# Adding a projection in DRAM, holding back query copies and reordering the first image in a list-scheduled attention kernel

## The chip, the cores and the metric

The kernel runs on one core of one Trainium2 chip. The metric is the device time of one execution in microseconds (us), the median of several runs. All profiled executions quoted here are of the fast state. Names: PE is TensorE (PEld its weight loads), DVE is VectorE, ACT is ScalarE, POOL is GpSimd, SP is SyncE, whose queue starts 406 of the 608 transfers that the profile of before lists. An "exp" is the ACT pass that turns one step's attention scores into probabilities.

How the profile's lines are read: L668 or L669 is the helper through which most instructions go, so the tiles tell what an instruction is. `sc` is the tile of the scores, `pt` a tile of probabilities, `sm` and `sx` the PSUM tiles of the background work, `kt` the keys on their way, `xr` the projection's row, `pool` the staging tile of the queries. A line such as `PE sc <- ACT pt: 114.0, 95, 7.1` says that PE, before instructions on `sc`, waited for ACT's on `pt`: us in total, times, longest.

## The reference, cut to what matters

```python
# x: 8 images, 256 channels, 32 x 32
# layer 0: on the group-normalised image
q  = 1x1 conv(x)                              # 8 heads of 32
kv = 1x1 conv(x)
pooled(t): for sides 32, 16, 11, 5: average pool, add depthwise 3x3   # 1426 tokens
k, v = layernorm(pooled(k_map)), layernorm(pooled(v_map))
out  = softmax(q k^T * scale) v               # 1024 queries x 1426 keys per head
out  = proj(mix(out)) + proj_b                # mix: a small 32 x 32 attention per head
x = x + out
# layer 1: attention over each image's 1024 tokens, then 8 experts of three products each
```

Layer 0 makes 384 steps of attention: 8 images, 2 groups of 4 heads, 2 halves of the queries, 12 chunks of keys.

## The kernel before: the parts that matter

The program orders its own instructions. While it is built, a small model of the engines (`Flow`) keeps the expected time of each engine and of each tile. The attention steps are the fixed backbone; convolutions, projections and layer 1 are background threads. A thread hands over what it needs next (`yield pe(tile, tag="sm")`: PE, these tiles ready, a PSUM tile free), and the model decides between which two attention steps the group goes. What it decides, the order of each engine's list, is fixed at build time.

```python
FILLER, PACE, PACE1, CAP, MARGIN, LANDING = 5, 4.0, 2.0, (1.5, 1.5), 1.5, 9.5

def note(...):                     # after every instruction: when will its output be there?
    lag = 0.15
    if "dma" in op:
        lag = 3.0 if engine == "SP" else LANDING
    ...

def runnable(self, need, rank=0):  # may this thread's next group go in here?
    ...
    return (not self.closed
            and (self.credit[rank >= FILLER] > 0 or pe < until - 0.5)
            and at + MARGIN <= until and slot <= until)

def scores(b, c, sl, kc):          # one attention step; ONE PSUM tile "sc", 6 tiles "pt"
    t = T(psum, [P, 4, 512], "sc")
    ... 4 matmuls ...
    pt = T(work, [P, 4, 512], "pt", bufs=6)
    f.act.activation(pt[:w], t[:w], AF.Exp, scale=SCALE0)

def project(b):
    for m in range(2):
        for half in range(2):
            xt = T(work, [P, 512], "xr")                          # one tile
            f.sp.dma_start(xt, x[b, m * P : (m + 1) * P, sl])     # image row in
            yield pe(atts[b, 0], atts[b, 1], tag="sm")
            ... 2 matmuls into ps ...
            yield ve(ps, xt)
            f.ve.scalar_tensor_tensor(xt, ps, bias[:, m:m+1], xt, ALU.add, ALU.add)
            f.sp.dma_start(t1[b][:, m, sl], xt)

# queries of images 2 to 8: product, copy by ACT into the one "pool" tile, store to DRAM
yield pe(xi, tag="sm")
ps = small()
... 2 matmuls ...
q = T(work, [P, 512], "pool")                                     # taken after the matmul
f.act.activation(q, ps, AF.Copy, scale=...)
f.sp.dma_start(hn[b][:, c, sl], q)
```

Every second step's probability tile is added to the one before it by an accumulating transfer of POOL (`pt<-pt`, 1024 KB, landing 7.3 us after its issue in before, median), and is free for a new exp only when that has landed: ACT stood 45.6 us in 15 places of before for it.

## Time and profile before

| | before |
|---|---|
| time, median of 4 runs | 3413.79 us (3412.46 to 3414.23) |
| PE idle, 0 to 160 us | 160 − 102.03 = 58.0 us |
| PE idle, 160 to 2052 us (rest of attention) | 1892 − 1761.12 = 130.9 us |
| first, ninth exp | 105.99, 162.72 us |

The stretches of the second and third row come from a table of stretches of the kernel before. The columns are the stretch, its length, busy us (with the number of instructions) of PE, PEld, DVE, ACT and POOL, the granted TensorE clock, DMA share and GB/s:

```profile
0.00:160.00 160.00, 102.03 (x366) 48.38 (x367) 98.75 (x253) 64.43 (x110) 42.16 (x64) 0.83 0.22 57
160.00:2052.00 1892.00, 1761.12 (x9918) 793.52 (x9917) 1424.95 (x2459) 1163.51 (x1385) 405.99 (x473) 0.97 0.59 133
```

PE is at work 93% of the second stretch, so there is no large hole to close: what can be gained lies in a start that is a third idle and in many small waits.

### The profile page before, as it was taken

What the parts mean: (1) busy time and instruction counts of PE and PEld (TensorE: products, weight loads), DVE (VectorE), ACT (ScalarE), POOL (GpSimd) and SP (SyncE); (2) the same over time, 40 slices, a digit from 0 to 9 for tenths busy, and PEclk for the clock granted to TensorE, in tenths of its full rate; (3) what the DMA queues carried; (4) which work ended last, traced back from release to release, by engine and by line L of the source; (5) the groups of instructions that cost most, each with busy time, mean ns of one, the idle gap of its engine ahead of it and who ended that gap; (6) DMA issues with size and microseconds to landing.
All of it is one profiled execution on the core that took longest, in us unless ns stands there. A gap on an engine that the chain in (4) does not pass through costs nothing.

```text
span 3418.4 us, 39922 instructions
## 1 busy us (share of the span) xinstructions
PE 3204.7 (94%) x15264; PEld 1781.8 (52%) x15264; DVE 2285.8 (67%) x3914; ACT 1675.6 (49%) x2193; POOL 499.0 (15%) x616
## 2 busy tenths in 40 slices
PE   7588899999999899999999989998999999999998
PEld 3232244444444334434434356646777777777776
DVE  6587798888888878888644543216776666666665
ACT  3466667566676576566664523342223333333332
POOL 3122213122141221321211200004000000000000
PEclk9699999999999999999999999999999999999999
DMA  1257565555555655555665663123440000000000
GB/s 48 63 114 165 135 135 115 125 126 123 138 116 122 161 108 128 127 122 129 148 134 132 141 191 124 56 77 132 140 160 31 19 29 27 19 19 19 19 13 20
DMA packets 105032, 337.47 MB, mean 99 GB/s; under 512 B 12976, under 2 KB 38328, under 8 KB 81600
## 3 DMA queue, kind: packets, MB, share of 16 engines
q0 software_dynamic: 24576, 172.51, 25.8%
q1 hardware_dynamic: 76896, 160.35, 13.6%
q8 instruction: 122, 2.00, 0.2%
q10 hardware_dynamic: 3360, 1.97, 0.2%
q14 instruction: 78, 0.64, 0.1%
HBM read 98.33 MB, written 63.97 MB: 47 GB/s over the span
## 4 chain that ended last, share of the span: by engine, by line
PE 74%; DMA 5%; ACT 4%; DVE 2%; issue 2%; POOL 1%; SPq 0%; ACTq 0%; DVEq 0%; POOLq 0%
PE bank L669 25%; PE sm L669 18%; PE y L669 11%; PE sc L669 8%; PE sx L669 6%; PE pv L669 6%; ACT pt L669 3%; DMA pt<-pt 2%; DMA t<-xr 1%; DMA xr<-in_x_dram 1%; DVE acc L669 0%; DMA hn<-hn 0%; DVE pt L669 0%; DVE rec L669 0%; DVE xr L669 0%
## 5 line engine op out<-in xcount | busy, mean ns | idle before, releaser
L669 ACT ACTIVATE pt<-sc 128x2048 f32<-128x2048 f32 (+1 forms) x384 | 720.7, 1877 | 317.1 <-PE sc L669 244.7
L669 PE MATMUL sc<-q,kn 32*128 32x512 f32 (+1 forms) x3072 | 452.4, 659 | 115.5 <-ACT pt L669 114.0
L669 DVE SCALAR_TENSOR_TENSOR acc<-p,vec,acc 128x225 f32<-128x225 f32 (+7 forms) x928 | 528.5, 576 | 35.7 <-ACT acc L669 11.2
L669 PE MATMUL bank<-h,w2e 128*128 128x512 f32 x1024 | 480.5, 595 | 0.0
L669 ACT ACTIVATE h<-bank,bnvec 128x512 f32<-128x512 f32 x302 | 233.1, 772 | 484.5 <-PE bank L669 464.4
L669 DVE TENSOR_TENSOR pt<-pt,pt 128x1024 f32<-128x1024 f32 x320 | 390.0, 1261 | 84.8 <-DMA pt<-pt 82.6
L669 PE MATMUL pv<-pt,vt 128*32 128x512 f32 (+1 forms) x3072 | 422.6, 623 | 0.0
L669 ACT ACTIVATE h<-c,bnvec 128x512 f32<-128x512 f32 x210 | 159.6, 807 | 318.6 <-DVE c L669 318.6
L669 POOL DMA_DIRECT2D pt<-pt x192 | 169.8, 884 | 923.2 <-ACT pt L669 788.8
L669 DVE TENSOR_TENSOR c<-p1c,bank 128x512 f32<-128x512 f32 x105 | 72.2, 688 | 314.9 <-PE bank L669 314.9
L669 PEld LDWEIGHTS sc<-q,kn 32*128 32x128 f32 (+1 forms) x3072 | 117.8, 181 | 311.5 <-ACT pt L669 209.4
L669 PEld LDWEIGHTS bank<-h,w2e 128*128 128x128 f32 x1024 | 194.8, 191 | 153.0 <-issue 141.4
L669 PEld LDWEIGHTS pv<-pt,vt 128*32 128x32 f32 (+1 forms) x3072 | 61.0, 109 | 306.6 <-issue 291.4
L669 POOL TENSOR_TENSOR rstd<-rstd,mhalf 128x4 f32<-128x4 f32 (+2 forms) x88 | 107.0, 1216 | 733.8 <-DVE rstd L669 593.7
L669 DVE TENSOR_TENSOR h<-h,gates 128x1024 f32<-128x1024 f32 x128 | 156.9, 1226 | 71.3 <-DMA h<-h 64.2
L669 PE MATMUL bank<-hn,w1e 128*128 128x256 f32 (+1 forms) x604 | 192.7, 448 | 10.1 <-DMA hn<-hn 10.1
L669 PE MATMUL y<-t,s3e 128*128 128x256 f32 x768 | 187.1, 380 | 0.0
L669 PE MATMUL sm<-p,v 128*128 128x256 f32 x736 | 173.8, 388 | 6.1 <-DVE xr L669 6.1
L669 ACT ACTIVATE p<-sm 128x512 f32<-128x512 f32 (+1 forms) x154 | 89.9, 584 | 173.7 <-PE sm L669 134.2
L669 PE MATMUL sm<-y,t 128*128 128x256 f32 x712 | 169.4, 385 | 2.1 <-ACT p L669 2.1
L669 PEld LDWEIGHTS bank<-hn,w1e 128*128 128x128 f32 x604 | 114.7, 191 | 99.9 <-issue 92.4
L669 PEld LDWEIGHTS sm<-p,v 128*128 128x128 f32 x736 | 139.3, 193 | 49.7 <-issue 24.4
(294 smaller groups left out, 4624.9 us busy)
## 6 DMA issues: line engine op xcount, KB each, us to landing
pt<-pt POOLq DMA_DIRECT2D x160, 1024.0 KB, 7.3
h<-h SPq DMA_DIRECT2D x80, 512.0 KB, 3.4
xi<-in_x_dram SPq DMA_DIRECT2D x16, 512.0 KB, 5.0
t<-t SPq DMA_DIRECT2D x8, 1024.0 KB, 6.9
res<-t SPq DMA_DIRECT2D x32, 256.0 KB, 4.4
t<-res SPq DMA_DIRECT2D x32, 256.0 KB, 2.6
hn<-res SPq DMA_DIRECT2D x32, 256.0 KB, 3.4
hn<-hn SPq DMA_DIRECT2D x16, 512.0 KB, 5.8
```

What stands on the lines that cost most here:

```text
L669: ins = fn(*args, **kwargs)
```

## The change

Its intent: (1) no engine waits for an image row to land, because the image is copied to its place in DRAM ahead of time and the projection is added to it there by a transfer; (2) a query product isn't started before its staging tile is free, so ACT doesn't stand behind a transfer; (3) the first scores come earlier: keys' maps first, their tiles taken from layer 1's space so that the probability tiles stay free; and the model's landing times are made to grow with the size of the transfer.

```diff
-LANDING = 9.5
 ...
-            lag = 3.0 if engine == "SP" else LANDING
+            size = 4e-3 * out.shape[0] * out.free_size() ...      # KB
+            lag = 2.0 + 0.0045 * size if engine == "SP" else 1.5 + 0.0078 * size
 ...
 def first_maps(xp):
-    for m in (2, 3, 0, 1):         # values first; maps 0 and 1 and a sum in "pt" tiles
+    for m in range(4):             # keys first; two "pt" tiles, sums in "kn" and layer 1's "v"
 ...
-    f.spawn(first_keys(), 5)       # all four key convolutions as one thread
+    f.spawn(first_keys(0), 1)
+    f.spawn(first_keys(1), 5)
 ...
 def prepare(b):
+    if b:
+        yield until(lambda: len(asked) == 4)
     xi = xs.pop(b) if b in xs else load_x(b)
+    if b < nb - 1:
+        f.sp.dma_start(t1[b], x[b].rearrange("(k p) n -> p k n", p=P))
 ...
 def queries(b, xi):
-    yield pe(xi, tag="sm")
+    q = T(work, [P, 512], "pool") if b else qs[b, c][:, sl]
+    yield pe(xi, q, tag="sm")
 ...
 def project(b):
-    f.sp.dma_start(xt, x[b, m * P : (m + 1) * P, sl])
-    yield pe(atts[b, 0], atts[b, 1], tag="sm")
+    yield pe(atts[b, 0], atts[b, 1], xt, tag="sm")
     ...
-    yield ve(ps, xt)
-    f.ve.scalar_tensor_tensor(xt, ps, bias[:, m : m + 1], xt, ALU.add, ALU.add)
-    f.sp.dma_start(t1[b][:, m, sl], xt)
+    yield act(ps)
+    f.act.activation(xt, ps, AF.Identity, bias=bias[:, m : m + 1])
+    yield pool(xt)
+    f.pool.dma_start(out=t1[b][:, m, sl], in_=xt, accum_op=ALU.add)
 ...
-f.finish(lambda: key_parts[0] > 1)                  # first score after two groups of keys
+f.finish(lambda: key_parts[0] > 0)                  # after one
 ...
+    if i == 4:                                      # fifth score: key maps' small taps must be placed
+        f.finish(lambda: {0, 1}.issubset(whole))
```

(Cut: the last image keeps the old projection; the queries of the first image are a thread of their own, and so are its groups of value tokens; the diagonals of the first convolutions and the projection weights move to other tiles of layer 1.)

More of the change, by code (lines that the diff above doesn't have):

```diff
@@ L783, in note @@
         if "dma" in op:
-            lag = 3.0 if engine == "SP" else LANDING
+            size = 4e-3 * out.shape[0] * out.free_size() if out.space != DRAM else 4e-3 * srcs[0].shape[0] * srcs[0].free_size()
+            lag = 2.0 + 0.0045 * size if engine == "SP" else 1.5 + 0.0078 * size
         for n in {*outs, self.key(out)}:
@@ L925, in attention @@
         gqkw = weight(gqk_t, "y", 512, l1)
-        pjw = weight(proj_t, "v", 256, l1)
+        pjw = T(l1, [P, 2, C], "p1", bufs=6)
+        nc.scalar.dma_start(pjw, proj_t.rearrange("(k p) f -> p k f", p=P))
         con = kit.con
@@ L1113, in attention @@
         f.split(pmap, 512, HW)
-        first, large, whole, pooled = {}, [], [], []
+        first, large, whole, pooled, asked = {}, [], [], [], []
         def first_diagonals():
             middle = T(l1, [P, 2, P], "rec1")
-            rest = T(work, [P, 4, 512], "pt", bufs=6).rearrange("p a (b q) -> p (a b) q", q=P)
+            rest = T(l1, [P, 16, P], "t")
             first["diag"] = middle, rest
@@ L1128, in first_maps @@
         def first_maps(xp):
-            for m in (2, 3, 0, 1):
-                c = m % 2
-                if m == 2:
-                    p, acc = pmap, T(work, [P, NK], "acc", bufs=3)
-                elif m == 3:
+            for m in range(4):
+                if m < 2:
                     p = T(work, [P, 4, 512], "pt", bufs=6).rearrange("p j q -> p (j q)")
+                    acc = T(l1, [P, NK], "v") if m else T(work, [P, NK], "kn", bufs=3)
+                else:
+                    p = T(work, [P, NK], "acc", bufs=3) if m == 3 else pmap
                     acc = T(work, [P, NK], "acc", bufs=3)
-                else:
-                    both = T(work, [P, 4, 512], "pt", bufs=6).rearrange("p j q -> p (j q)")
-                    p = both
-                    acc = T(work, [P, 4, 512], "pt", bufs=6).rearrange("p j q -> p (j q)")
                 for t in (p, acc):
@@ L1145, in first_maps @@
                 first[m] = p, acc
-            for s0, w in KEY_SLICES:
-                if s0 >= HW:
+            for m, s0 in [(m, s0) for g in (0, 2) for s0 in (0, 512) for m in (g, g + 1)] + [(m, HW) for m in range(4)]:
+                if s0 == HW:
                     yield until(lambda: pooled)
-                for m in (2, 3, 0, 1):
-                    c = m % 2
-                    p, acc = first[m]
-                    src = source(xp, s0, w)
-                    yield pe(src, tag="sm")
-                    ps = small()
-                    for k in range(2):
-                        f.pe.matmul(
-                            ps[:, :w],
-                            lhsT=kvw[:, k, m * P : (m + 1) * P],
-                            rhs=src[:, k, :],
-                            start=k == 0,
-                            stop=k == 1,
-                        )
-                    f.act.activation(p[:, s0 : s0 + w], ps[:, :w], AF.Copy)
-                    for s, n in enumerate(SIDES):
-                        a, z = max(OFFS[s], s0), min(OFFS[s] + n * n, s0 + w)
-                        if a < z and (m >= 2 or s):
-                            f.act.activation(
-                                acc[:, a:z],
-                                ps[:, a - s0 : z - s0],
-                                AF.Identity,
-                                bias=db(c, s),
-                                scale=mid[:, c * 4 + s : c * 4 + s + 1],
-                            )
-                if s0 == 512:
@@ new lines, in first_maps @@
+                w = min(512, NK - s0)
+                c = m % 2
+                p, acc = first[m]
+                src = source(xp, s0, w)
+                yield pe(src, tag="sm")
+                ps = small()
+                for k in range(2):
+                    f.pe.matmul(
+                        ps[:, :w],
+                        lhsT=kvw[:, k, m * P : (m + 1) * P],
+                        rhs=src[:, k, :],
+                        start=k == 0,
+                        stop=k == 1,
+                    )
@@ new lines, in first_maps @@
+                f.act.activation(p[:, s0 : s0 + w], ps[:, :w], AF.Copy)
+                for s, n in enumerate(SIDES):
+                    a, z = max(OFFS[s], s0), min(OFFS[s] + n * n, s0 + w)
+                    if a < z and (m >= 2 or s):
+                        f.act.activation(
+                            acc[:, a:z],
+                            ps[:, a - s0 : z - s0],
+                            AF.Identity,
+                            bias=db(c, s),
+                            scale=mid[:, c * 4 + s : c * 4 + s + 1],
+                        )
@@ L1175, in first_maps, with first_keys @@
+                if (m, s0) == (3, 512):
                     large.append("maps")
-                    f.spawn(first_keys(), 5)
+                    f.spawn(first_keys(0), 1)
+                    f.spawn(first_keys(1), 5)
             whole.append("maps")
-        def first_keys():
+        def first_keys(half):
             n = SIDES[0]
             middle, rest = first["diag"]
-            for half in range(2):
-                for m in range(2):
-                    p, acc = first[m]
-                    pin = p[:, : n * n].rearrange("p (h w) -> p h w", h=n)
-                    yield pe(p[:, : n * n], middle, rest, tag="sm")
-                    ps = small()
-                    pout = ps.rearrange("p (h w) -> p h w", w=n)
-                    for i, tap in enumerate((4, 0, 1, 2, 3, 5, 6, 7, 8)):
-                        dy, dx, y0, y1, x0, x1 = windows(tap, n)
-                        y0, y1 = max(y0, 16 * half), min(y1, 16 * half + 16)
-                        f.pe.matmul(
-                            pout[:, y0 - 16 * half : y1 - 16 * half, x0:x1],
-                            lhsT=rest[:, 8 * m + i - 1, :] if i else middle[:, m, :],
-                            rhs=pin[:, y0 + dy : y1 + dy, x0 + dx : x1 + dx],
-                            start=i == 0,
-                            stop=i == 8,
-                        )
-                    f.act.activation(acc[:, half * 512 : half * 512 + 512], ps, AF.Identity, bias=db(m, 0))
-                large.append(("keys", half))
@@ new lines, in first_keys @@
+            for m in range(2):
+                p, acc = first[m]
+                pin = p[:, : n * n].rearrange("p (h w) -> p h w", h=n)
+                yield pe(p[:, : n * n], middle, rest, tag="sm")
+                ps = small()
+                pout = ps.rearrange("p (h w) -> p h w", w=n)
+                for i, tap in enumerate((4, 0, 1, 2, 3, 5, 6, 7, 8)):
+                    dy, dx, y0, y1, x0, x1 = windows(tap, n)
+                    y0, y1 = max(y0, 16 * half), min(y1, 16 * half + 16)
+                    f.pe.matmul(
+                        pout[:, y0 - 16 * half : y1 - 16 * half, x0:x1],
+                        lhsT=rest[:, 8 * m + i - 1, :] if i else middle[:, m, :],
+                        rhs=pin[:, y0 + dy : y1 + dy, x0 + dx : x1 + dx],
+                        start=i == 0,
+                        stop=i == 8,
+                    )
+                f.act.activation(acc[:, half * 512 : half * 512 + 512], ps, AF.Identity, bias=db(m, 0))
@@ L1203, in taps @@
+            large.append(("keys", half))
         def taps(c, s, p, acc):
@@ L1376, in prepare @@
                 todo.extend([None] * 4)
+                f.spawn(queries(b, xi), 3)
                 yield from first_maps(xp)
@@ L1379, in prepare, with queries @@
                 yield from maps(xp)
+            if b:
+                yield from queries(b, xi)
+            made[0] += 1
+        def queries(b, xi):
             for c in range(2):
@@ L1395, in prepare @@
                         )
-                    q = T(work, [P, 512], "pool") if b else qs[b, c][:, sl]
                     f.act.activation(q, ps, AF.Copy, scale=vec[:, V_NW + c : V_NW + c + 1])
@@ L1399, in prepare @@
                         f.sp.dma_start(hn[b][:, c, sl], q)
-            made[0] += 1
+                    else:
+                        asked.append((c, half))
         def fetch_queries():
@@ L1440, in keys_and_values @@
             vts[b] = {}
-            if b == 0:
-                for g in range(2):
-                    yield from value_tokens(b, g)
-            else:
-                for g in range(3):
-                    f.spawn(value_tokens(b, g), 2)
+            for g in range(3):
+                f.spawn(value_tokens(b, g), 2)
+            if b:
                 yield until(lambda: len(vts[b]) == 3)
@@ L1449, in keys_and_values @@
                 yield until(lambda: len(done) >= 4 * b + 4)
-            for g in range(2 if b == 0 else 3):
+            for g in range(3):
                 yield from key_tokens(b, g)
             if b == 0:
-                yield from value_tokens(b, 2)
-                yield from key_tokens(b, 2)
+                yield until(lambda: len(vts[b]) == 3)
                 freed[0] += 1
@@ L1520, in project @@
                     sl = slice(half * 512, half * 512 + 512)
-                    if b == nb - 1:
-                        xt = last[:, m, sl]
-                    else:
-                        xt = T(work, [P, 512], "xr")
-                        f.sp.dma_start(xt, x[b, m * P : (m + 1) * P, sl])
-                    yield pe(atts[b, 0], atts[b, 1], tag="sm")
+                    xt = last[:, m, sl] if b == nb - 1 else T(work, [P, 512], "xr")
+                    yield pe(atts[b, 0], atts[b, 1], xt, tag="sm")
                     ps = small()
@@ L1531, in project @@
                         )
-                    yield ve(ps, xt)
-                    f.ve.scalar_tensor_tensor(xt, ps, bias[:, m : m + 1], xt, ALU.add, ALU.add)
-                    if b < nb - 1:
-                        f.sp.dma_start(t1[b][:, m, sl], xt)
+                    if b == nb - 1:
+                        yield ve(ps, xt)
+                        f.ve.scalar_tensor_tensor(xt, ps, bias[:, m : m + 1], xt, ALU.add, ALU.add)
+                    else:
+                        yield act(ps)
+                        f.act.activation(xt, ps, AF.Identity, bias=bias[:, m : m + 1])
+                        yield pool(xt)
+                        f.pool.dma_start(out=t1[b][:, m, sl], in_=xt, accum_op=ALU.add)
             if b == nb - 1:
@@ L1815, in attention @@
                 if (half, kc) == (0, 0):
-                    f.finish(lambda: (b, c) in qs)
+                    f.finish(lambda: (b, c) in qs and (b or (c, 0) in asked))
                     turn[0] = 2 * b + c
                     atts[b, c] = T(work, [P, HW], "att", bufs=2)
+                if i == 4:
+                    f.finish(lambda: {0, 1}.issubset(whole))
+                if b == 0 and kc == 0:
+                    f.finish(lambda: (c, half) in asked)
                 pts[i] = scores(b, c, sl, kc)
```

## The prediction

> **What bounds the kernel now.** I read the page first: TensorE (PE) is busy 3204.7 of 3418.4 us (94%), VectorE (DVE) 67%, ScalarE (ACT) 49%, and the chain that ended last is PE for 74% of the span. So the time is PE work plus PE idle, and the question is where PE's 214 us of idle lie. The second view is the table of stretches; columns are the stretch, its length, busy us of PE, PEld, DVE, ACT, POOL, then granted clock, DMA share and GB/s.
>
> ```profile
> 0.00:85.00 85.00, 62.20 (x168) 30.49 (x168) 55.71 (x118) 32.38 (x69) 26.95 (x44) 0.97 0.15 48
> 85.00:171.00 86.00, 50.83 (x236) 22.58 (x236) 45.40 (x139) 38.63 (x51) 15.21 (x21) 0.70 0.29 63
> ...
> 1026.00:1368.00 342.00, 323.17 (x1797) 147.89 (x1795) 282.40 (x519) 216.64 (x273) 75.17 (x87) 0.99 0.58 130
> ...
> 2394.00:3418.00 1024.00, 1010.39 (x3876) 735.85 (x3874) 642.88 (x1002) 334.08 (x521) 0.00 (x0) 0.99 0.12 43
> ```
>
> The first 171 us hold 58 us of PE idle, at a clock of 0.70 in the second half. From about 340 us PE is 92 to 96% busy, and the experts after 2394 us, which the change doesn't touch, leave 14 us. The third view is who PE waited for:
>
> ```profile
> PE sc L669 <- ACT pt L669: 114.0, 95, 7.1
> PE sx L669 <- ACT kt L669: 12.5, 1, 12.5
> PE sm L669 <- DVE xr L669: 12.3, 3, 6.1
> PE sm L669 <- ACT kt L669: 11.3, 3, 6.4
> ...
> PE sm L669 <- ACT pool L669: 2.3, 1, 2.3
> ```
>
> The first row is mostly not a fault to be mended here: the scores have one PSUM tile, so a step of attention takes score 1.1 us plus exp 1.88 us plus handover, 3.15 us, and where nothing is put between, PE idles 1.0 us. I counted such bare steps in the order of PE's instructions: 64 of 384 before, 65 after. That part stays.
>
> How the start looks, in order of time:
>
> ```profile
> 105.99 1.88 ACT L669 ACTIVATE pt<-sc 128x2048 f32<-128x2048 f32 x1
> 128.35 1.88 ACT L669 ACTIVATE pt<-sc 128x2048 f32<-128x2048 f32 x1 [6.43 <-DMA pt<-pt]
> 134.01 1.88 ACT L669 ACTIVATE pt<-sc 128x2048 f32<-128x2048 f32 x1 [3.64 <-DVE pt L669]
> 143.87 1.88 ACT L669 ACTIVATE pt<-sc 128x2048 f32<-128x2048 f32 x1 [7.98 <-DMA pt<-pt]
> 162.72 1.88 ACT L669 ACTIVATE pt<-sc 128x2048 f32<-128x2048 f32 x1 [1.43 <-PE sc L669]
> ```
>
> These are the first, fifth, sixth, seventh and ninth exp. The first image's maps fill the six probability tiles, so exps wait for tiles. The ninth needs the third group of keys, which needs all small convolution taps on DVE. And the two waits that the change names, a projection and a query copy:
>
> ```profile
> 1367.91 0.75 DVE L669 SCALAR_TENSOR_TENSOR xr<-sm,mtb,xr 128x512 f32<-128x512 f32 x1 [2.94 <-DMA xr<-in_x_dram]
> 1368.72 3.78 PE L669 MATMUL sm<-xi,qw 128*128 128x512 f32 x4 [6.00 <-DVE xr L669]
> ...
> 287.05 0.69 ACT L669 ACTIVATE pool<-sm,vec 128x512 f32<-128x512 f32 x1 [2.67 <-DMA hn<-pool]
> 287.64 1.87 ACT L669 ACTIVATE pt<-sc 128x2048 f32<-128x2048 f32 x1
> 289.56 1.14 PE L669 MATMUL sc<-q,kn 32*128 32x512 f32 x8 [2.05 <-ACT pt L669]
> ```
>
> In the first, DVE stands at the head of its queue until the image row has landed, the PSUM tile stays taken, PE stands 6.00 us. In the second, ACT stands until the one staging tile has left, the exp behind it is late, PE stands 2.05 us.
>
> [...] This trace has only accumulates in SBUF (the probability tiles: 1024 KB, 7.3 us to landing); none into DRAM, so that cost is my estimate. [...] here the DMA share is 0.56 to 0.62 in most of attention, so there is room. [...] granted clock 0.70 in the stretch with idle gaps of 12.5, 7.1, 6.4 and 6.4 us. [...]
>
> **The change, part 1: projection in DRAM.** It removes 28 additions on DVE (0.745 us each, 20.9 us), 28 loads of 256 KB and 28 stores, and adds 28 ACT copies with bias (an ACT pass over 128x512 with scale takes 0.69 us: 19.3 us), 28 GpSimd issues (0.86 us each as for the probability tiles: 24 us on an engine busy 15%) and 7 copies of 1 MB from DRAM to DRAM. The copies are issued one image ahead, on the sync queue. Bytes stay the same: the copy replaces the load, the accumulate the store. An accumulated byte takes more engine time: 25.8% of the span for 172.51 MB against 13.6% for 160.35 MB, 1.8 times as much per byte; 7.3 MB of it is about 1% of the span, off the path. On PE's path lies only the wait: 12.3 us (6.1 + 6.0 + 0.2). DVE's 20.9 us is beside PE and frees little; ACT's 19.3 us lands on an engine busy 63% there and can delay an exp by 0.7 us now and then, of 28 perhaps a third on the path, 5 us. Net −12.3 + 5 = about −7, −12 at best.
>
> **Part 2, queries held back.** ACT waited 38.1 us in 16 places for the staging tile. I laid these beside PE's gaps of over 0.3 us: PE stood in four places, 2.05, 0.42, 2.33 and 0.68 us, 5.5 us. All of it should go, since the matmul is now not issued before the tile is expected free: −5.
>
> **Part 3, the start.** By the order of instructions. PE now does four query and eight map groups first: 12 × 1.72 us (four matmuls at 0.43) from 14.35, to 35. Then two convolutions of 7.4 us, to 50. DVE starts its 16 large taps (1.27 us) at 35 instead of 26, has 15 done at 54, then the first keys' statistics, the second image's statistics, and the 16th tap at about 63.5. The value transposes wait for that, then the last key convolution (7.4 us) ends at 73, ACT normalises the keys behind it, transposes, first score at about 78, first exp after two table loads (2.6 us) at about 81 instead of 106.
>
> But that is not the gain. Four exps then go without waiting for a tile; the sixth and seventh take the tiles of the key maps and wait for DVE's taps, as the waits in the built program confirm. DVE's small taps took from 52.25 to 133.9 before, 81.7 us. After, that stretch loses a statistics chain (3.6 us) and about 6 us of waits, and takes in layer 1's weight preparation (4.5 us of copies and scalings, 8.0 us for the batch norm vectors with their GpSimd waits): 84.6 us, from 63.5 to 148. Behind it come the third keys' transposes, one sum of 2.35 us, statistics, normalisation, transposes, some 13 us: the ninth exp at about 161 to 163, against 162.72. What is gained is what PE did by then: eight groups of layer-1 weight products (1.9, 2.0, 0.95, 0.95, 2.0 and three of 1.9 us, 13.4 us) stand before the ninth score now, and stood behind it, in a stretch where PE was full (9.0 and 10 of 10 us from 170 to 190). DVE gets a similar lead. So −14, and the first score 25 us earlier mostly buys idle time.
>
> **Sum.** −7 −5 −14 = −26; better landing estimates (2.7 instead of 9.5 us for the 18-row adds, 6.7 instead of 3.0 for large loads) should take a few of the 16 us in which PE stood because an exp waited for a tile's DMA (2.8 to 3.9 us each): −3. 3413.5 − 29 = 3384.
>
> **Rivals.** (a) The first score's 25 us arrive whole at the end: for it, PE idles 58 us there and the clock is low; against it, the tap count on DVE is the same and DVE must finish before the ninth exp. It would give about 3360. (b) The waits on xr only change place: layer 1's load of t1 must wait for the last accumulate, GpSimd's queue holds the probability adds behind an accumulate that waits for ACT, and the one xr tile now serialises four chunks. For it, one tile and a queue in order; against it, chunks are spread and layer 1 is filler. It would leave part 1 at zero or +8: 3392 to 3400. (c) The 1 MB copy, issued right behind the first image, slows the first weights: landing near 9.4 us, needed at 14.35; a miss costs 1 to 4 us. (d) The reordering of some 1,500 us of background work is luck of ±8 us either way.
>
> **Range and chances.** Good: −24 −12 −6 −10 = 3362. Bad: −3 −6 −2 = 3402. 2% is 68 us, 39% of the 175 us of idle before 2052 us that isn't the first load; I give that 4%. Slower by 2% has no mechanism: 1%.
>
> **What would show it.** First exp near 81, sixth and seventh waiting for DVE, ninth near 162; layer-1 weight products before 160 us; no PE wait on DVE xr, and under 3 us on its successor; ACT's wait for the staging tile under 8 us; PE idle from 400 to 2000 us down by 10 to 20 us; total PE busy unchanged within 20 us. I am wrong if the ninth exp comes 15 us earlier (rival a), if exps wait longer for tiles because accumulates crowd the adds, or if PE waits at the load of t1.

## The result, and the profile after

| | before | after |
|---|---|---|
| time, median of 4 runs each | 3413.79 us | 3382.82 us (3382.07 to 3386.29) |
| ratio | | 0.9912 (0.9895 to 0.9929) |
| PE idle, 0 to 160 us | 58.0 us | 43.6 us |
| PE idle, 160 to 2052 us | 130.9 us | 113.9 us |

A ratio is the mean time of one kernel's fast runs over the mean of the other's in the same rounds, so it is not quite the ratio of the medians.

The result is 31.0 us faster, 0.9%, well clear of the noise; predicted were 29. (It is less than 2%, which the record's class calls "same"; the prediction gave this 95%.) The idle of PE before 2052 us fell by 14.4 + 17.0 = 31.4 us. That this is so near to 31.0 is chance: the two profiled executions differ by 38.5 us (spans of 3418.4 and 3379.9 us; that of before took 3420.16 us, 6 us above its median), of which PE's idle in the whole span is 28.8 us and its busy time 9.7 us. The table of stretches of the changed kernel, columns as before:

```profile
0.00:160.00 160.00, 116.40 (x436) 60.65 (x440) 100.52 (x268) 67.42 (x117) 45.12 (x66) 0.86 0.28 76
160.00:2052.00 1892.00, 1778.15 (x10005) 806.47 (x9998) 1420.32 (x2458) 1191.58 (x1427) 428.76 (x505) 0.98 0.61 133
```

PE does 14.4 us more before 160 us. ACT has 28 us more in the second stretch, mostly its 28 copies of the projection; POOL has 23 us more, the issues of the new adds.

The exps of the start, in order of time (start, duration, engine, operation, tiles, and in brackets how long ACT stood idle before and for what): first, fifth, sixth, seventh, ninth.

```profile
82.01 1.88 ACT L668 ACTIVATE pt<-sc 128x2048 f32<-128x2048 f32 x1
...
143.83 1.88 ACT L668 ACTIVATE pt<-sc 128x2048 f32<-128x2048 f32 x1 [0.67 <-PE sc L668]
146.97 1.88 ACT L668 ACTIVATE pt<-sc 128x2048 f32<-128x2048 f32 x1 [1.26 <-PE sc L668]
...
151.79 1.88 ACT L668 ACTIVATE pt<-sc 128x2048 f32<-128x2048 f32 x1 [0.46 <-PE sc L668]
...
161.53 1.88 ACT L668 ACTIVATE pt<-sc 128x2048 f32<-128x2048 f32 x1 [1.30 <-PE sc L668]
```

The first exp comes 24 us earlier and the ninth 1.2 us earlier. Between the fourth (93.44 us) and the fifth lie 50 us. The sixth and seventh don't wait for DVE here; they wait for their own scores.

Who PE waited for, in us in total, times, and the longest:

```profile
PE sc L668 <- ACT pt L668: 92.9, 96, 3.2
...
PE sx L668 <- DVE rec L668: 8.0, 1, 8.0
...
PE sm L668 <- DVE p L668: 6.7, 2, 6.0
PE sx L668 <- DMA res<-in_w_dram: 4.7, 1, 4.7
PE sm L668 <- ACT kt L668: 4.3, 9, 1.5
PE sx L668 <- ACT kt L668: 3.6, 5, 2.9
```

The waits on the projection's row (`DVE xr`, 12.3 us) are gone, and so is the one on the query copy (`ACT pool`, 2.3 us). PE's waits for ACT's work on the keys (`ACT kt`), the largest of the old start, fell from 12.5 + 11.3 to 3.6 + 4.3 us. Three new ones are in the start: PE stands at groups of the mixing matrix (`rec`, `p`) and of layer 1's weights (`res`) that its order puts ahead of the fifth score. And what touched the projection's tile:

```profile
L668 POOL DMA_DIRECT2D t<-xr x28: 863/882/931, 346.5 to 1810.8; - x28
...
  POOL t L668: 113.7, 23
  PEld sc L668: 0.2, 1
...
DMA to landing us min/median/max: 4.3/4.7/5.8
```

The first row is POOL's issues (ns, minimum, median, maximum; first and last start). The next two are who waited for an instruction on this tile: POOL stood 113.7 us for ACT's copies, but none of these issues is in the chain of work that ended last, and PE's weight loads lost 0.2 us. The add of 256 KB into DRAM lands after 4.7 us.

Of the signs that I named, two are missing: the sixth and seventh exp, and the idle of PE from 400 to 2000 us, which fell by 7.4 us (82.0 to 74.6) and not by 10 to 20. The second is partly a matter of the window: in after it takes in PE's wait before the experts' first products (10.98 us, ending at 1997.70 us), which in before ends at 2014.84 us. The other signs are there. It remains to be seen whether each part of the change gives what I put down for it.

### The profile page after: what moved, and what is told of

Read it like the earlier page. It is cut to its first block, busy times and chain, and to the rows that moved or that the text cites. A ratio compares the mean times of both kernels' runs of the same rounds, so it can differ in the third digit from the quotient of the medians.

```text
span 3379.9 us, 39921 instructions
## 1 busy us (share of the span) xinstructions
PE 3195.0 (95%) x15270; PEld 1780.3 (53%) x15270; DVE 2267.8 (67%) x3890; ACT 1695.4 (50%) x2222; POOL 520.7 (15%) x644
## 3 DMA queue, kind: packets, MB, share of 16 engines
q10 hardware_dynamic: 3360, 1.97, 0.2%
## 4 chain that ended last, share of the span: by engine, by line
PE 66%; ACT 2%; issue 2%; DMA 1%; DVE 1%; POOL 1%; SPq 0%; POOLq 0%; ACTq 0%; DVEq 0%
PE bank L668 25%; PE sm L668 14%; PE y L668 11%; PE sc L668 6%; PE sx L668 6%; PE pv L668 5%; ACT pt L668 2%; DMA pt<-pt 1%; POOL rstd L668 0%; DVE t L668 0%; DMA h<-h 0%; DMA hn<-hn 0%; POOL pt L668 0%; DVE rec L668 0%; DMA t<-pt 0%
## 5 line engine op out<-in xcount | busy, mean ns | idle before, releaser
L668 PE MATMUL sc<-q,kn 32*128 32x512 f32 (+1 forms) x3072 | 444.8, 649 | 94.2 <-ACT pt L668 92.9
L668 PE MATMUL sm<-y,t 128*128 128x256 f32 x752 | 180.4, 385 | 0.0
L668 PEld LDWEIGHTS sm<-y,t 128*128 128x128 f32 x752 | 137.9, 190 | 56.1 <-issue 34.4
L668 PE MATMUL bank<-t,s1e 128*128 128x256 f32 x636 | 154.7, 379 | 2.8 <-DVE t L668 2.8
```

Source lines behind the costliest of these rows:

```text
L668: ins = fn(*args, **kwargs)
```

## The experiments

Twelve kernels were run, in three groups; each group ran on one chip beside the kernel before, whose medians were 3414.8, 3413.4 and 3413.6 us. Theory A is the prediction: each part has its own gain and the gains add up (−7, −5, −14, −3). Theory B is my rival (d), made larger: where the background groups fall is luck, and worth more than the parts. Theory C is that the parts move waits to other places.

### One part alone

`e1_dram_only`: the kernel before with the changed `project` and the copy in `prepare`, and

```diff
-            lag = 3.0 if engine == "SP" else LANDING
+            lag = 3.0 if engine == "SP" else 3.5 if out.space == DRAM else LANDING
```

This second line was needed. With 9.5 us put down for the new adds, too, the model placed the projection so late that a check of the built program found the attention tile read after a later image's had replaced it. The landing estimates are thus no separate nicety: part 1, as it is written here, can't be built safely on the old one.

> The kernel before with part 1 alone (projection copied by ACT, added to the image in DRAM; the old landing estimates stay, except 3.5 us for the new adds into DRAM). My prediction gives -7 us, so about 3406.5 us, with PE's 12.3 us of waits on the image row gone and first exp unchanged near 106 us. Rival (b), the wait only changes place: 3413 to 3421 us. Rival (d), reordering is luck: anything within 8 us of 3413.5, and PE's idle moves in stretches where no projection stands.

Measured: 3414.02 us against 3414.8, ratio 0.9998 (0.999 to 1.0006). PE's waits on the image row are gone, and nothing is gained. In the profile PE idles 126.6 us from 160 to 2052 us (before: 130.9).

`e2_held_only`: the kernel before with

```diff
-                    yield pe(xi, tag="sm")
+                    q = T(work, [P, 512], "pool") if b else qs[b, c][:, sl]
+                    yield pe(xi, q, tag="sm")
                     ...
-                    q = T(work, [P, 512], "pool") if b else qs[b, c][:, sl]
```

> The kernel before with part 2 alone (query copies of images 2 to 8 issued when the staging tile is free). Prediction: ACT's 38.1 us of waits for the staging tile fall under 8 us, PE gains 5 us: about 3408.5 us. Rival: the waits were off the path, 3412 to 3415 us with ACT's wait still gone. Rival (d), luck: up to 8 us either way.

Measured: 3456.30 us, ratio 1.0124: 42 us slower. ACT's wait for the staging tile is 0, as expected, so the part does what it is meant to do. What it costs is not at that tile: PE idles 150.8 us from 160 to 2052 us, 20 us more than before, at waits in many places (image rows 19.0 us instead of 12.3, layer 1's load of the image 11.4 instead of 2.1). (The window leaves out this kernel's wait before the experts' first products, 6.1 us, and holds that of before, 10.1 us; without these two it is 30 us more.)

`e3_start_only`: the changed kernel with the old `project`, `queries` and landing estimates, so the kernel before with part 3 alone.

> The kernel before with part 3 alone (keys first, other tiles for the first image's maps, split first keys; old landing estimates, old projection, queries not held). Prediction: first exp near 82 us, ninth near 162 us, -14 us in all: about 3399.5 us, with PE idle before 160 us down by 14 us. Rival (a), the first exp's 24 us arrive whole: about 3388 us. Rival: the products of layer 1 moved ahead were free before as well, then 3410 to 3414 us.

Measured: 3418.28 us, ratio 1.001 (1.0003 to 1.0017). Its table of stretches:

```profile
0.00:160.00 160.00, 118.13 (x444) 60.89 (x448) 101.06 (x269) 67.85 (x118) 45.05 (x66) 0.86 0.25 65
160.00:2052.00 1892.00, 1753.21 (x9880) 786.50 (x9873) 1436.46 (x2450) 1159.30 (x1380) 401.57 (x471) 0.98 0.58 130
```

First exp 81.3 us, ninth 159.9. In its own stretch the part gives 16.1 us of PE idle (58.0 − 41.9), as predicted. In the rest PE idles 138.8 us, 7.9 more than before, and no gain is left at the end.

`e4_landing_only`: the kernel before with the two new `lag` lines alone.

> The kernel before with the new landing estimates alone. Prediction: -3 us, about 3410.5 us, and ACT waits less for probability tiles whose add has not landed (45.6 us in 15 places before). Rival: this is the larger part of what came from 400 to 2000 us, -10 us or more, 3403 us or less. Rival (d), luck: within 8 us either way, with that wait unchanged.

Measured: 3430.17 us, ratio 1.0045 (1.0033 to 1.0058), 15 us slower. The exps' waits for a tile whose add had not landed did fall, from 29.4 to 24.2 us from 160 to 2052 us. PE's idle in that stretch rose to 148.4 us.

Four parts that are each 0 to 42 us slower by themselves, and 31 us faster together: theory A doesn't hold in its simple form. Either the parts need each other, or something else decides between kernels of this kind.

### Nothing of the change: neighbours

To see what placing alone does, I changed a number that is no property of the chip: `MARGIN`, by which an operand must be expected ready before its group is put between two scores. The order of PE's instructions in the built program is then the same for a stretch at its beginning and another from there on.

```diff
-MARGIN = 1.5
+MARGIN = 1.4        # n_before_14, n_after_14;  1.6 in n_before_16, n_after_16
```

> The kernel before with nothing of the change; the margin by which an operand must be ready before a group is put between two scores goes from 1.5 to 1.4 us, which means nothing for the hardware but puts most of the background work in other places. Theory 'the placing is luck and before stood on a lucky one': 10 to 40 us slower, 3424 to 3455 us, as e2 (+42) and e4 (+15) were. Rival 'each part of the change has its own cost, placing is worth under 8 us': 3406 to 3421 us.

> The same with 1.6 us. Luck theory: 3424 to 3455 us. Rival: 3406 to 3421 us. If one neighbour is faster than before by more than 5 us, before was not a lucky placing.

> The changed kernel with the same margin 1.4 us. If the change has a gain of its own and before and after are equally tuned, this neighbour is as far above 3382.8 us as before's neighbours are above 3413.5 us (gap of the means of neighbours 20 to 35 us). If after is only a lucky placing, it falls among before's neighbours, at 3415 us or more. If placing is worth little, 3375 to 3391 us.

> The changed kernel with 1.6 us. The same three outcomes: a gap to before's neighbours of 20 to 35 us (own gain), none (luck), or 3375 to 3391 us (placing worth little).

Measured:

| kernel | time, us | PE idle 0 to 160 | PE idle 160 to 2052 | span profiled | PE busy in it |
|---|---|---|---|---|---|
| before | 3413.4 | 58.0 | 130.9 | 3418.4 | 3204.7 |
| n_before_14 | 3427.9 | 57.8 | 126.4 | 3431.6 | 3220.7 |
| n_before_16 | 3453.8 | 57.9 | 165.3 | 3455.7 | 3210.8 |
| after | 3382.8 | 43.6 | 113.9 | 3379.9 | 3195.0 |
| n_after_14 | 3404.3 | 43.3 | 128.0 | 3400.6 | 3202.9 |
| n_after_16 | 3385.3 | 42.9 | 106.8 | 3380.4 | 3206.1 |

The time is a median; the other columns are of one profiled execution. After itself wasn't run again in this group.

The tenth of a microsecond that means nothing costs 14.5 and 40.4 us beside before, and 21.5 and 2.5 us beside after. Each of the two kernels is the fastest of its three. The table of stretches of the slowest, n_before_16, and then who its PE waited for:

```profile
0.00:160.00 160.00, 102.09 (x367) 48.26 (x367) 98.69 (x253) 64.62 (x110) 41.93 (x64) 0.83 0.23 57
160.00:2052.00 1892.00, 1726.68 (x9762) 763.51 (x9761) 1418.69 (x2425) 1153.56 (x1365) 406.36 (x469) 0.97 0.57 128
```

```profile
PE sc L669 <- ACT pt L669: 134.0, 111, 7.1
...
PE sx L669 <- DMA t<-t: 10.9, 3, 4.9
...
PE sx L669 <- POOL tst L669: 6.1, 1, 6.1
```

The start is the same to 0.1 us. Behind it PE does 34 us less in the same time. It waits at more scores for the exp before (111 times against 95, 20 us more). Attention steps with no background group between them explain little of that: in the built programs there are 67 against 64. A few groups stand at a worse place: PE waits 10.9 us in three places of one PSUM tile for layer 1's image load (and 4.2 us in one of the other), and 6.1 us for POOL's `tst`. Behind the start no one of these waits is longer than 6.1 us; it is their sum that is large.

Idle is not all. n_before_14 has 2.8 us less PE idle in its whole span than before and is still 13.2 us longer in the profile: PE is busy 16.0 us more, with practically the same products to do. In the six kernels this busy time differs by up to 26 us. The granted clock is 0.972 to 0.974 in the profiles of before's three and 0.977 to 0.980 in those of after's, and the profiles of before and after hold 15264 and 15270 matmuls; what makes the difference has not been followed.

The families don't overlap: the three placings of before have the mean 3431.7 us, those of after 3390.8. The gap is 40.9 us. Between the profiled executions it is 48.3 us, of which the start's stretch holds 14.6 (mean idle 57.9 against 43.3), the rest of attention 24.6 (140.9 against 116.2) and PE's busy time 10.7. The standard deviations are 20.5 and 11.8 us, so three against three gives the gap with a standard error of about 14 us (the root of a third of the sum of their squares), and a 95% interval would reach down to about zero. Theory B in its strong form, the change is only a lucky placing, is unlikely by this; the kernels of the next group make it weaker still. But of the single comparisons of one kernel with another, those above included, none under some 20 us says much.

### All but one part

`e5_no_dram` (the changed kernel with the old `project`, without the copy), `e7_no_held` (the tile `q` taken after the matmul again), `e8_no_start` (the kernel before with parts 1, 2 and the estimates).

```diff
 # e5: as the change's diff of project and prepare, reversed
 # e7
-                    q = T(work, [P, 512], "pool") if b else qs[b, c][:, sl]
-                    yield pe(xi, q, tag="sm")
+                    yield pe(xi, tag="sm")
                     ...
+                    q = T(work, [P, 512], "pool") if b else qs[b, c][:, sl]
 # e8: first_maps, first_keys, keys_and_values, the tiles and the finish conditions as before
```

> The changed kernel without part 1 (projection added by DVE, image rows loaded, no copy of 1 MB). If part 1 has a gain of its own of 7 us or more, this stands above the mean of after and its two neighbours (3382.8, 3404.3, 3385.3; mean 3391): 3398 us or more, with PE waits of 5 to 13 us on the image row back, which the three kernels without part 1 have (12.3, 4.8, 7.0 us) and the three with it have not. If part 1 gives nothing, it lies between 3380 and 3405 us like those three.

Measured: 3395.34 us, 4.5 above the mean of the after family. PE waits on the image row are back, 1.6 + 2.7 = 4.3 us. By what was put down beforehand that is the outcome for no gain (3380 to 3405 us); but a gain of that size would fit the spread as well.

> The changed kernel without part 2 (query copies issued before the staging tile is free). ACT's waits for that tile come back, 38 to 54 us as in all kernels without it. If they cost what I predicted, PE stands 2 to 5 us for them and the time is 5 us above the mean of 3391 us; if the many late exps behind them cost more, 15 us or more above, 3406 us or later; if nothing, 3380 to 3405 us.

Measured: 3403.74 us, 12.9 above the family's mean and within its range. ACT's waits (engine, tile, releaser, us, times, longest) are back:

```profile
ACT pool L668 <- DMA hn<-pool: 43.5, 17, 6.5
```

PE itself stood 2.8 + 0.2 us for that tile. The 5 us of the prediction and the 13 of the time can't be told apart at this spread.

> The changed kernel without part 3 (parts 1 and 2 and the new landing estimates on the kernel before). First exp near 106 us and PE idle before 160 us near 57 us, as in all kernels with the old start (54 to 58), against 43 in all with the new. Time 14 us above the mean of 3391 us, 3405 us, give or take the placing (20 us); idle from 400 to 1800 us as in the three changed ones (52 to 64 us) if the rest of the gain comes from parts 1 and 2 and the estimates, 66 us or more (as in the kernels of before, 66 to 107) if it comes with the start.

Measured: 3388.30 us, 2.5 *below* the family's mean. This was my largest miss in the expectations. The first exp is at 107.16 us, as in all with the old start, but the stretch reads otherwise:

```profile
0.00:160.00 160.00, 115.74 (x442) 54.98 (x443) 107.56 (x261) 75.05 (x122) 43.52 (x65) 0.88 0.28 75
160.00:2052.00 1892.00, 1767.08 (x9969) 807.15 (x9968) 1418.68 (x2448) 1185.14 (x1421) 434.14 (x502) 0.98 0.61 134
```

PE idles 44.3 us before 160 us, as little as with the new start. The ninth exp is what moved:

```profile
139.11 1.88 ACT L668 ACTIVATE pt<-sc 128x2048 f32<-128x2048 f32 x1 [2.16 <-PE sc L668]
...
145.03 1.88 ACT L668 ACTIVATE pt<-sc 128x2048 f32<-128x2048 f32 x1 [0.62 <-PE sc L668]
```

It comes at 145.03 instead of 162.72 us. In the kernel before, the fifth and seventh exp stood 6.43 and 7.98 us for a tile's add to land, and DVE's last small tap ended at 133.9 us; here the waits of the fifth to eighth are at most 2.16 us (the fourth waits 5.67 us for DVE), the taps end at 122.6 us, and DVE stands less (busy 107.6 us before 160 us, against 98.8). Which moved group began it I have not followed. The estimates alone don't do it (e4: ninth exp at 163.7 us, idle 55.2 us). So the start's 14 us can be had in two ways, by more work before a ninth exp at 162 us (part 3) or by an earlier ninth exp with the old start. With parts 1, 2 and the estimates there, part 3 gives nothing that these runs show; but this is one placing, so only to some 20 us. The idle from 400 to 1800 us, the other thing that was put down, is 62.0 us, inside the 52 to 64 of the three changed kernels (before: 69.0); e5 and e7 have 65.9 and 66.8, so it does not tell the parts apart.

### What the start's gain is made of

`e12_weights_late`: the changed kernel with the mixing matrix and layer 1's weights begun after the third group of keys.

```diff
-f.spawn(chain(mix(), weights1(), outputs()), 5)
-f.spawn(layer1(), 6)
     ...
+                if i == 8:
+                    f.spawn(chain(mix(), weights1(), outputs()), 5)
+                    f.spawn(layer1(), 6)
```

> The changed kernel with the mixing matrix and layer 1's weight products begun only after the third keys are there. DVE then has none of their work and waits between 88 and 137 us (about 10 us of work, 13 us of waits), so the ninth exp should come near 138 us instead of 161.5. My prediction says that the start's gain is the PE work done before the ninth score: then this is a wash, the 20 us of PE work move behind it, PE idle before the ninth score stays 40 to 44 us, and the time is that of after give or take the placing (3375 to 3410 us). Rival (a), an earlier ninth exp is worth its whole time: 3360 to 3365 us, and this is the faster kernel. Rival: the ninth exp stays near 160 us because something else holds it, then 3400 us or more.

Measured: 3400.31 us. The ninth exp:

```profile
143.52 1.88 ACT L668 ACTIVATE pt<-sc 128x2048 f32<-128x2048 f32 x1
```

Its PE up to the end of the ninth score (columns as in the tables of stretches):

```profile
0.00:142.00 142.00, 94.42 (x348) 41.78 (x350) 96.01 (x233) 62.90 (x108) 39.49 (x64) 0.88 0.27 73
```

The exp is 18.0 us earlier than after's (I had expected 23), and the time is 9.5 us above the family's mean, within its range. PE idles 47.6 us up to the ninth score, where 40 to 44 were expected (after: 43.6 in 160 us), and 49.2 us before 160 us. An earlier ninth exp is not worth its own length: rival (a) asked for 3360 to 3365 us. The time to the ninth exp shrinks by what DVE no longer does, and PE has as much less done by then: 94.4 us of work in 142 us, where after's PE has done 116.4 us in 160. This is about the wash that the prediction's view of the start implies. It is also the one candidate for a faster kernel that these readings suggested, and it isn't faster. The fastest kernels measured are the changed one and its neighbour n_after_16.

### What was not run

What this paragraph says of builds is the author's account; the record holds no run of them. The direct rival to part 1, the old addition with the matmul held until the image row has landed, didn't pass the check of races with one row tile, and the build had no room for two; a mended form passed but was not among the twelve. The changed kernel with the old landing estimates (and 3.5 us for the new adds) was built and not run either. Nor were kernels with two of the four parts, or neighbours of those with one.

## Why the prediction was right, point by point

**The total.** 3384 us predicted, 3382.8 measured. The 14 us of the start are seen where they were predicted. The other 15 are not shown part by part, and that the sum came within 1.2 us is partly luck: against the families' means the gap is 41 ± 14 us, with which the predicted 29 agree. Had the change been made with the neighbour's 1.4 us, its 3404.3 us would have been 20 us from my number and outside my range.

**What bounds the kernel.** Held. PE's waits for the exp at scores from 160 to 2052 us were 94.2 us in 89 places and are 89.3 in 91. Bare steps stayed, as counted.

**Part 1, −7.** The wait is gone in all kernels with it (0 us), and is 2.4 to 19 us in those without, on the sum of both PSUM tiles, by placing. It only partly changed place: POOL stands 113.7 us, outside the chain that ended last. As time it is not shown: alone 0, left out 4.5 us slower, both within the spread. (One term of its sum was reckoned low: a third of 28 delays of 0.7 us is 6.5 us, not 5, which would have made the part about −6.) Rival (b) doesn't show either; PE's wait at layer 1's load is 2.7 us against 2.1, though that load lands later (1 MB after 9.3 us instead of 6.9, median of 8). Rival (c) doesn't show: PE's wait ahead of the first map product is 1.9 us in both.

**Part 2, −5.** ACT's 38.1 us went to 0, better than the "under 8" predicted. PE's own stand for it was 5.5 us before by my count and 3.0 us in e7. As time it isn't shown: alone 42 us slower, left out 13 us slower than the mean, the first of which no wait on that tile explains.

**Part 3, −14.** In its stretch it measured 14.4 us (first exp 82.01 for 81 predicted, ninth 161.53 for 161 to 163, DVE's taps ending at 147.4 for 148), and 14 to 16 us in every kernel with it but e12 (8.8). The gain is, as I said, what PE does before a ninth exp that hardly moves; e12 supports it. The step that failed is "the sixth and seventh take the tiles of the key maps and wait for DVE's taps". The program places all those taps before the fifth score, and with them the mixing matrix and layer 1's weights on PE, so the *fifth score* is issued only at 142.41 us, when the taps are nearly done, and nobody is seen waiting. The size of the stretch was the same either way. What I didn't see at all is that the gain is neither safe once earned (e3 gives it back) nor reserved to this part (e8).

**Landing estimates, −3.** The exps' waits for landing tiles went from 29.4 to 16.6 us from 160 to 2052 us in the changed kernel, but they are 30.5 and 32.0 us in its neighbours. The estimates do not reliably shorten them. Nor are all of them near what was measured: by its formulas the model now expects 2.7 us for the 18-row adds (4.5 measured in the changed kernel, median), 3.5 for the adds into DRAM (4.7) and 6.7 for the copies from DRAM to DRAM (13.9); for adds of 128 rows it expects 9.7 (7.4).

**Rival (d), ±8 us.** This term was mis-sized. It measured up to 40 us beside before and 21 beside after, more than any part. My sum treated it as noise around the parts; it is the largest term.

**What stays open.** How the 41 us split among the four parts. A least-squares fit of a constant and one effect for each part to thirteen kernels (all but e12) gives −18, −1, −13 and −14 us for parts 1, 2, 3 and the estimates, each with a standard error of 11 to 13 us: nothing can be told apart. Kernels with one part have the mean 3429.7 us, like before's family; those with three or four 3395.8 and 3390.8. That looks like parts that need company, but with such a spread I can only say so, not show it. What the fourteen kernels do show together is a gain of the whole: all seven with none or one of the parts took 3413.4 us or more, all seven with three or four (e12 with them) 3404.3 us or less.

## What to carry to other kernels

When a program places its own background work, measure a few neighbours of both kernels that differ in a number without meaning, before believing any difference smaller than their spread. A prediction of the total can come true while the experiments can't confirm its terms. A wait that has vanished from the profile is proof of the mechanism, not of the time; check whether the idle of the bounding engine fell over the whole stretch, since what one place gains the next placing can give back. Both kernels here were the fastest of their three placings; where that is so, undoing a part of a change also loses the lucky placing, and the time lost isn't that part's alone.
